# Moving normalization statistics, one normalization chain and two groups of loads in a fused deformable-convolution and mixture-of-experts kernel

## The chip, the cores and the metric

The kernel runs on one core of one Trainium2 chip. Time is the device time of one execution in microseconds (us); each version is run several times and the median is compared. The core has five engines that run side by side and wait for each other through semaphores: PE (TensorE, matmuls), DVE (VectorE), ACT (ScalarE), POOL (GpSimd) and SP (SyncE, which here only issues DMA transfers). ACT and POOL issue DMA transfers too.

## The reference, cut to what matters

Two layers on eight images of 128 channels and 64 x 64 pixels, float32. Before each layer the image is group-normalized (32 groups of 4 channels, no learned scale), and each layer's result is added to its input.

```python
# layer 0: deformable 3x3 convolution, then batch norm and relu
om = conv(_gn(x), off_w)                 # 27 maps: 9 y offsets, 9 x offsets, 9 masks
py, px = grid + offsets                  # per tap, pixel: where to sample
val = bilinear(_gn(x), py, px) * sigmoid(mask)
y = einsum('bckhw,ock->bohw', val, w) + b
x = x + relu(batch_norm(y) * gamma + beta)     # mean, var over all images
# layer 1: 4 experts, 2 chosen per image, plus a shared expert, each a 3x3 convolution
x = x + sum_e w_dense[b, e] * conv(_gn(x), expert_w[e]) + conv(_gn(x), shared_w)
```

The change touches layer 0 alone, which takes about the first 1060 us.

## The kernel before, in words

**Bands.** Each image is cut into 8 bands of 8 rows, 64 bands in all, counted by `g` through all images (`b, j = bands[g]`). The bilinear sampling is done with matrices: for each band two tables of weights, one by y offset and one by x offset, are multiplied (`weights`, L865, on DVE) to a matrix `s`; PE multiplies the transposed pixels with it (`sample`, L881, five groups per band, 12 matmuls each, so 60 in a timeline row are a whole band and 36 the three groups that PE can run ahead); ACT copies the sampled values out of PSUM (L891). PE can be three groups ahead of ACT's copies, since three PSUM buffers hold them; five `s` buffers let DVE be a band ahead of PE. Iteration `g` of the main loop first does the sampling of band `g` and then the 3x3 convolution of band `g - 1`, nine taps (L931), and between two taps it issues small pieces of everything else. A "tap" or `part` below is such a place, 0 to 8.

**Tables.** The weights come from the image's offsets. `tables(b)` is a generator that produces them for image `b`, one small step per `tick()`: four ticks per tap in the first eight iterations, three afterwards. It has two halves. The first is the normalization chain: `mv` (mean and variance per channel, made by `statistics`) goes through a matmul `pm` over the groups (L318), then on DVE `d`, `e` (L323) and `gm`, a second matmul `pv` (L328), `ve` on DVE (L333), the power −0.5 on POOL (`scale`, L336), `shift` on DVE (L339), and then the image is normalized in place in eight chunks (`pad`, L343 on ACT, L347 on DVE). The second half computes the offset convolution, writes its result to DRAM, loads it back turned by rows and by columns (ten row loads, L568; column loads, L554), nudges it (L611), forms distances (L615 for y, L626 for x), makes weights out of them with ACT (L636, L640) and a mask multiply on DVE (L673), and stores the x table (`store_x`, L591, six transfers) and the y table (`store_y`, L663) in DRAM. From there every band fetches its own part with broadcasting loads: `load_x(g)` is two transfers of 576 KB (L754), `load_y(g)` eight transfers of 36 to 144 KB (L735). These loads are issued by POOL, in the order of the program, except in the head. `spread` (L773 on ACT, L779 on DVE) turns the loaded x distances into weights. Three buffers rotate for each of the two tables.

**Statistics.** `statistics(b)` is a second generator: eight `bn_stats` (L303), one per chunk of 8 rows, and after the last one `bn_aggr` (L306), which gives `mv`. In iteration `8b + 4` it is started for image `b + 2`, whose rows are loaded by quarters (`load_quarter`) in iterations `8b + 1` to `8b + 4`. In iteration `8b + 5` what is left of the tables of image `b + 1` is run through (`for _ in made: pass`), and the chain for image `b + 2` begins.

**The head.** Up to about 95 us the tables of image 0 and the first bands are made, outside the main loop. There the loads are spread over SP, ACT and POOL. `load_y(0)` goes on SP (k = 3, 5), ACT (k = 4, 6) and POOL (the others); the y table is stored in two pieces, rows for the first band (`soon`) ahead of the loads and the rest behind them; so is the x table. `y_wts` are three y-weight buffers that must be zeroed once; the first two memsets stand earlier, the third at L990 behind `load_y(1)`.

**Order.** Each engine runs its instructions in program order. Waits are inserted by the framework from the buffers that are read and written; each DMA transfer also waits for the one before it on its lane, of which there are eight for SP and ACT together and eight for POOL.

Of the kernel before, what the change touches and what calls it, by code (L numbers as in the profile page):

```python
# [46 lines left out]
NB = NROW // 2  # L47
# [18 lines left out]
def deform_moe_conv(  # L66
# [18 lines left out]
    nc = tc.nc  # L85
    B = x.shape[0]
# [9 lines left out]
        out=gsel, in_=gsel, compare_op=ALU.is_ge, fill=0.0, base=0,  # L96
# [3 lines left out]
        out=gsel, in_=gsel, compare_op=ALU.is_ge, fill=0.0, base=3,  # L100
# [79 lines left out]
    def dense():  # L180

        with ExitStack() as st:
# [12 lines left out]
            for t in pads:  # L195
# [16 lines left out]
                out=ident, in_=ident, compare_op=ALU.is_equal, fill=0.0, base=0,  # L212
# [6 lines left out]
            for i, at in ((0, 0), (1, H - 1)):  # L219
                for half in (slice(0, W), slice(W, P)):  # L220
                    nc.gpsimd.affine_select(
                        out=nudge[half, i : i + 1], in_=nudge[half, i : i + 1],
# [16 lines left out]
            for base, sign, fill in ((-W - REACH, 1, -REACH), (P - 1 - REACH, -1, T + REACH)):  # L239
                nc.gpsimd.affine_select(  # L240
                    out=beside, in_=beside, compare_op=ALU.is_ge, fill=float(fill), base=base,
# [9 lines left out]
            raw_off = combos[1].rearrange("p h w -> p (h w)")[:, OFF_AT : OFF_AT + 18 * W].rearrange(  # L251
                "p (v t n) -> p v t n", v=3, t=2
            )
# [6 lines left out]
            y_wts = [a1.tile([P, T, 3, W, 3], F32, name=f"ywts{i}") for i in range(3)]  # L260
# [11 lines left out]
            def pause(n):  # L272
                for _ in range(n):
                    yield
# [34 lines left out]
            def tables(b):  # L309
# [4 lines left out]
                part = chunks(b)  # L314
# [42 lines left out]
                even, odd = two[:, :, 0], two[:, :, 1]  # L357
# [167 lines left out]
                for j in range(4):  # L525
                    (nc.sync if b or j % 2 == 0 else nc.scalar).dma_start(
                        out=rowwise[b][:, H // 4 * j : H // 4 * (j + 1)].rearrange(
                            "s h w -> s (h w)"
                        ),
                        in_=omr[32 * j : 32 * j + 27],  # L530
                    )
                for j in range(4):
                    (nc.sync if b or j % 2 else nc.gpsimd).dma_start(
                        out=colwise[b][:, :, j].rearrange("k u w h -> u k (w h)"),
                        in_=om[32 * j + 9 : 32 * j + 18, 1],
# [9 lines left out]
                by_row = rowwise[b].rearrange("(t k u) h w -> k h t u w", t=3, k=3)  # L545
# [3 lines left out]
                by_column = []  # L549
# [9 lines left out]
                for k in range(3):  # L559
                    lo, hi = max(0, k - 1), min(H, H + k - 1)  # L560
                    places = [(slice(lo, hi), slice(lo + 1 - k, hi + 1 - k), k)]
                    if k == 2:
                        places.append((slice(0, 1), slice(0, 1), 0))
                    if k == 0:
                        places.append((slice(H - 1, H), slice(H - 1, H), 2))
                    for outs, parts, v in places:
                        for t in range(2):
                            (nc.sync if b or t == 0 else nc.scalar).dma_start(  # L568
                                out=raw_off[parts, v, t].rearrange("p (u w) -> p u w", u=3),
                                in_=by_row[k][outs, 2 * t],  # L570
                            )
                        by_column.append((k, outs, parts, v))
                if b:
                    yield from pause(27)
                for k, *where in by_column:
# [127 lines left out]
                for k, halves in ((3, 2), (4, 2), (5, 2), (6, 2), (1, 2), (2, 2), (0, 1), (7, 1)):  # L703
                    engine = {3: nc.sync, 5: nc.sync, 4: nc.scalar, 6: nc.scalar}.get(k, nc.gpsimd)
                    for h in range(halves):
                        load_y(0, k, engine, (h,) if halves == 2 else (0, 1))
                load_x(1, nc.gpsimd)
                store_y(0, NR, slice(4 * T, H))
                store_x(4, NROW, nc.sync)
                pick(1)  # L710
# [37 lines left out]
            def load_x(g, engine):  # L748

                if g >= len(bands):  # L750
                    return
                b, j = bands[g]
                for h in range(2):
                    engine.dma_start(  # L754
                        out=x_wts[g % 3][HALF * h : HALF * h + HALF],
                        in_=bass.AP(
                            tensor=x_table[b].tensor,
                            offset=x_table[b].offset + (2 * j + h) * XROW,
                            ap=[[0, HALF], [1, XROW]],
                        ),  # L760
                    )
# [225 lines left out]
            HALVES = (0, EVEN), (EVEN, NCOL + 1)  # L987
            for k in range(2 * T):
                load_y(1, k, nc.gpsimd)
            nc.gpsimd.memset(y_wts[2], 0.0)  # L990
            load_x(2, nc.gpsimd)
            made, means_of = later, iter(())
            asked = False
# [27 lines left out]
            for g in range(len(bands) + 1):  # L1021
                b, j = bands[g] if g < len(bands) else (B, 0)
                if j == NB - 4:
                    means_of = statistics(b + 2)
                turned = pixels(g + 2)
                if j == NB - 2:
                    tick()
                for q in range(NGR):
                    if g < len(bands):
                        sample(g * NGR + q)  # L1030
                        if g:
                            weights(g * NGR + q + AHEAD)
                        if g == 0 and q == 2:
                            for k in range(Q):
                                load_y(2, k, nc.gpsimd)
                    if g == 0 and q == 1:
                        for _ in range(4):
                            next(later)
                    if q == 1:
                        put_off()  # L1040
                taps = conv(g - 1) if g else iter(())
                twice = 2 if g and bands[g - 1][1] == NB - 1 else 1
                for done, _ in enumerate(taps):
                    part, odd = divmod(done, twice)
                    if odd == 0 and part in PIXELS:
                        next(turned, None)
                    if odd == 0 and part == 2:
                        load_x(g + 3, nc.gpsimd)
                        if g < len(bands):
                            edges(g)  # L1050
                    if odd == 0 and part > 6:
                        for k in range(T * (part - 7), T * (part - 6)):
                            load_y(g + 3, k, nc.gpsimd)
                    if odd == 0 and part in SPREAD:
                        step, half = divmod(SPREAD.index(part), 2)
                        if step:
                            spread(g + 2, HALVES[half], ())
                        else:
                            spread(g + 2, sides_=(half,), clip=False)
                    if odd == 0 and part in SHARE:  # L1060
                        piece = SHARE.index(part)
                        share(g + 2, piece, MOVES[piece])
                    if odd == 0 and j == NB - 4 and part > 4:
                        next(means_of, None)
                    if odd == 0 and j == NB - 3 and part < 2:
                        for _ in range(2):
                            next(means_of, None)
                    if odd == 0 and j == NB - 3 and part == (4 if b else 7) and b + 2 < B:
                        for _ in made:
                            pass  # L1070
                        asked, made = True, tables(b + 2)
                        next(made)
                    if odd == 0 and part in BLOCKS and asked:
                        asked = False
                        tick()
                    for _ in range(3 + (g < NB) if twice == 1 else 1 + done % 2):
                        tick()
                    if odd == 0 and part == 4:
                        pick(g + 3)
                        if 2 <= j < 5:  # L1080
                            load_quarter(b + 2, j - 1)
                    if odd == 0 and part == 8 and j == 1:
                        load_quarter(b + 2, 0)
                if g == 0:
                    edges(0)
                    spread(1)
                    for n in range(AHEAD):
                        weights(NGR + n)
                for _ in turned:
                    pass  # L1090
                if g == 0:
                    for piece in range(4):
                        share(2, piece, MOVES[piece])
                    load_x(3, nc.gpsimd)
                    for k in range(Q):
                        load_y(3, k, nc.gpsimd)
                    pick(3)
                    spread(2)
                if g == 3:
                    quad_weights()  # L1100
                if j < NB - 1 and g < len(bands):
                    late.append((hand_on, g))
                xts.pop(g - 1, None)
                if j == 1 and b:
                    nc.vector.bn_aggr(ymvs[:, b - 1], ystats[:, b - 1])
                if (b, j) == (B - 1, 1):
                    reach()
# [596 lines left out]
```

## Time and profile before

| | us |
|---|---|
| median of 3 runs | 1431.47 |
| the runs | 1428.11, 1431.47, 1432.19 |
| profiled execution | 1432.73 |
| its span on the core | 1431.0 |
| PE busy / DVE busy / ACT busy / POOL busy in it | 1291.0 / 1063.3 / 835.0 / 471.6 |

The mean TensorE clock that was granted is 0.966 of full speed in the profiled execution. Times in the text are microseconds from the start of the span. In a timeline a row is a run of equal instructions on one engine: start, duration of the run, engine, line, operation, output and inputs, count, and in brackets how long the engine was idle before it and what ended that wait. The bracket is the place where lost time becomes visible; it costs something only on the engine that others wait for.

### The profile page before, as it was taken

The numbers are of one execution on the slowest core, as the hardware profiler recorded it, in microseconds if no ns is written. First come the engines' busy times: TensorE is split into PE (matmuls) and PEld (weight loads), VectorE is DVE, ScalarE is ACT, GpSimd is POOL, SyncE is SP. The second block draws the span as 40 slices with busy tenths as digits, with TensorE's granted clock in tenths as the row PEclk, the third lists the DMA queues.
The fourth block names the chain that finished last, engine by engine and source line by source line (L and its number), as shares of the span: only waits on it lengthen the run. The fifth ranks groups of instructions, "written<-read, shape, count | busy, mean of one in ns | idle before, by whom it ended". The sixth has DMA issues, their size and how long they took to land.

```text
span 1431.0 us, 21255 instructions
## 1 busy us (share of the span) xinstructions
PE 1291.0 (90%) x7561; PEld 731.3 (51%) x7561; DVE 1063.3 (74%) x2124; ACT 835.0 (58%) x1110; POOL 471.6 (33%) x750
## 2 busy tenths in 40 slices
PE   4169989999989999999998999999957999999998
PEld 1044556556656655665565565666533444444443
DVE  5658778679688778968877886746439887778972
ACT  2355866876787687688678668767623333322320
POOL 6354145335416424552552553255021110101000
PEclk9589999999999999999999999999988999999999
DMA  4589678968978887896898887689236644456411
GB/s 144 112 180 201 129 183 203 214 149 188 203 175 187 189 202 157 192 220 149 186 207 184 174 204 159 152 218 219 79 119 175 172 128 122 134 160 177 103 53 54
DMA packets 149429, 234.54 MB, mean 164 GB/s; under 512 B 101677, under 2 KB 104890, under 8 KB 139074
## 3 DMA queue, kind: packets, MB, share of 16 engines
q0 software_dynamic: 79408, 137.37, 44.4%
q1 hardware_dynamic: 69154, 95.15, 23.7%
q8 instruction: 61, 1.00, 0.3%
q10 hardware_dynamic: 752, 0.59, 0.2%
q14 instruction: 54, 0.44, 0.1%
HBM read 180.23 MB, written 45.35 MB: 158 GB/s over the span
## 4 chain that ended last, share of the span: by engine, by line
PE 54%; DMA 15%; DVE 10%; issue 9%; ACT 7%; SPq 3%; POOL 2%; DVEq 0%; ACTq 0%; POOLq 0%
PE py L931 20%; PE pc L1616 15%; PE pq L881 11%; PE pc L456 3%; DMA combo<-colwise 3%; DMA combo<-rowwise 3%; PE pt L822 3%; DMA xwts<-tabx 2%; DVE stats L303 2%; ACT xwts L773 2%; SPq L554 2%; DMA x<-in_x_dram 1%; DVE s L865 1%; DMA taby<-work 1%; DMA ywts<-taby 1%
## 5 line engine op out<-in xcount | busy, mean ns | idle before, releaser
L931 PE MATMUL py<-samples,dw_sb 128*128 128x512 f32 (+3 forms) x1296 | 561.1, 566 | 10.5 <-ACT y L939 10.5
L735 POOL DMA_DIRECT2D ywts<-taby x510 | 325.8, 656 | 386.8 <-DMA xwts<-tabx 172.4
L931 PEld LDWEIGHTS py<-samples,dw_sb 128*128 128x128 f32 x1296 | 229.8, 191 | 210.9 <-issue 175.8
L881 PE MATMUL pq<-s,xt 64*128 64x144 f32 (+1 forms) x3840 | 280.0, 299 | 35.6 <-ACT samples L891 26.7
L891 ACT COPY samples<-pq 128x864 f32<-128x864 f32 (+1 forms) x318 | 278.5, 973 | 31.4 <-PE pq L881 31.0
L881 PEld LDWEIGHTS pq<-s,xt 64*128 64x128 f32 x3840 | 254.2, 189 | 83.1 <-ACT samples L891 30.1
L865 DVE TENSOR_TENSOR s<-xwts,ywts 128x432 f32<-128x432 f32 (+1 forms) x448 | 198.6, 498 | 52.7 <-PE pq L881 41.6
L1616 PE MATMUL pc<-v,u 128*128 128x512 f32 x384 | 174.1, 600 | 6.4 <-DVE v L1523 6.3
L1616 PE MATMUL pc<-v,wmix 128*128 128x512 f32 x384 | 173.2, 596 | 0.0
L773 ACT ACTIVATE xwts<-xwts,place 128x1152 f32<-128x1152 f32 (+3 forms) x132 | 153.1, 1163 | 10.4 <-DMA xwts<-tabx 8.5
L779 DVE TENSOR_SCALAR xwts<-xwts 128x1152 f32<-128x1152 f32 (+2 forms) x128 | 96.0, 751 | 82.9 <-ACT xwts L773 82.8
L1594 ACT ACTIVATE t<-pc,bmix 128x512 f32<-128x512 f32 x32 | 22.0, 687 | 187.5 <-PE pc L1616 98.9
L754 POOL DMA_DIRECT2D xwts<-tabx x128 | 77.3, 620 | 157.1 <-DMA tabx<-combo 48.8
L939 ACT ACTIVATE y<-py,db_sb 128x512 f32<-128x512 f32 (+3 forms) x72 | 45.8, 636 | 130.0 <-PE py L931 122.9
L1616 PEld LDWEIGHTS pc<-v,u 128*128 128x128 f32 x384 | 71.8, 191 | 93.1 <-issue 83.1
L1616 PEld LDWEIGHTS pc<-v,wmix 128*128 128x128 f32 x384 | 71.9, 189 | 90.7 <-issue 89.0
L825 ACT COPY xt<-pt 128x512 f32<-128x512 f32 x126 | 74.0, 587 | 61.3 <-PE pt L822 51.3
L822 PEld LDWEIGHTS pt<-ident,picked 128*128 128x128 f32 x504 | 58.6, 141 | 91.5 <-ACT xt L825 40.3
L822 PE MATMUL pt<-ident,picked 128*128 128x128 f32 x504 | 77.8, 277 | 23.4 <-DVE picked L788 18.4
L788 DVE COPY picked<-pad 128x512 f32<-128x512 f32 x128 | 71.8, 603 | 31.2 <-PE pt L822 31.1
L838 DVE COPY xt<-xt 32x896 f32<-32x896 f32 x126 | 77.5, 615 | 2.8 <-ACT xt L825 1.2
L1012 DVE BATCH_NORM_STATS2 ystats<-y 128x6 f32<-128x512 f32 (+3 forms) x72 | 44.2, 622 | 23.7 <-ACT y L939 23.7
(209 smaller groups left out, 1168.0 us busy)
## 6 DMA issues: line engine op xcount, KB each, us to landing
xwts<-tabx POOLq DMA_DIRECT2D x128, 576.0 KB, 8.0
pad<-in_x_dram SPq DMA_DIRECT2D x36, 512.0 KB
ywts<-taby POOLq DMA_DIRECT2D x126, 144.0 KB, 9.5
out_dram<-yo SPq DMA_DIRECT2D x32, 512.0 KB
ywts<-taby POOLq DMA_DIRECT2D x126, 108.0 KB, 9.1
yd<-y SPq DMA_DIRECT2D x48, 256.0 KB
ywts<-taby POOLq DMA_DIRECT2D x126, 72.0 KB, 8.4
pad<-yd SPq DMA_DIRECT2D x16, 512.0 KB
```

What stands on the lines that cost most here:

```text
L735: engine.dma_start(out=y_wts[g % 3][HALF * h + k : HALF * (h + n) : Q, first : last + 1].rearrange("p r a b c -> p (r a b c)"), in_=bass.A ...
L754: engine.dma_start(out=x_wts[g % 3][HALF * h : HALF * h + HALF], in_=bass.AP(tensor=x_table[b].tensor, offset=x_table[b].offset + (2 * j + ...
L773: nc.scalar.activation(some, some, AF.Abs, bias=columns[side])
L779: nc.vector.tensor_scalar(some, some, -1.0, 0.0, ALU.add, ALU.min)
L822: nc.tensor.transpose(pt[:, c - c0], one.rearrange("p h x y -> p (h x y)"), ident)
L825: (nc.vector.tensor_copy if turn_odd else nc.scalar.copy)(xts[g][:, c0 : c0 + n], pt[:, 0:n])
L838: move(out=xts[g][rows, EVEN:].rearrange("p c n -> p (c n)"), in_=xts[g][rows, 1 - side : EVEN - side].rearrange("p c n -> p (c n)"),)
L865: nc.vector.tensor_tensor(s[:, :, 3 * at : 3 * (at + k)].rearrange("p m (c x) -> p m c x", x=3), by_x[:, :, c : c + k], by_y[:, :, w : w + ...
L881: nc.tensor.matmul(by_m[:, h, :, at : at + k], lhsT=xts[g][rows, c // 2 + EVEN * (c % 2)], rhs=s[rows, :, at : at + k], start=True, stop=True,
L891: (nc.scalar.copy if g or q < 3 else nc.vector.tensor_copy)(bass.AP(tensor=one.tensor, offset=one.offset + first, ap=[list(one.ap[0]), [M ...
L931: nc.tensor.matmul(py, lhsT=dw_sb[:, 3 * (2 - yy) + 2 - xx], rhs=samples[g % 2][:, m : m + 3 * n - 2 : 3, xx, 1 : W + 1], start=(i == 0), ...
L1616: nc.tensor.matmul(pc, lhsT=us[j][:, kx], rhs=vs[g][:, rows, kx : kx + W], start=(kx == 0), stop=(kx == 2),)
```

## The change

Three edits. In the row loads (L568) the list of places is made first; then the loads are issued with all the `t = 0` halves ahead of all the `t = 1` halves, and in the head they alternate between SP and ACT by place. Before, each place's two halves were issued together, `t = 0` on SP and `t = 1` on ACT; for later images all ten are on SP in both versions. In the head, `load_x(1)` moves from POOL to SP, where it follows SP's loads of y and precedes the remaining stores, and the memset of the third y-weight buffer moves from behind `load_y(1)` to the place that `load_x(1)` had. In the main loop, six of the eight statistics are issued in iteration `8b + 4` (taps 1 to 6) and two in iteration `8b + 5` (tap 0), where it was four (taps 5 to 8) and four (taps 0 and 1); and the chain of image 2 (`b` = 0) begins at tap 4, as those of the other images already did, and not at tap 7.

```diff
                     for outs, parts, v in places:
-                        for t in range(2):
-                            (nc.sync if b or t == 0 else nc.scalar).dma_start(
-                                out=raw_off[parts, v, t].rearrange("p (u w) -> p u w", u=3),
-                                in_=by_row[k][outs, 2 * t],
-                            )
                         by_column.append((k, outs, parts, v))
+                queues = (nc.sync, nc.sync if b else nc.scalar)
+                for n, t in ((n, t) for t in range(2) for n in range(len(by_column))):
+                    k, outs, parts, v = by_column[n]
+                    queues[n % 2].dma_start(
+                        out=raw_off[parts, v, t].rearrange("p (u w) -> p u w", u=3),
+                        in_=by_row[k][outs, 2 * t],
+                    )
...
-                load_x(1, nc.gpsimd)
+                nc.gpsimd.memset(y_wts[2], 0.0)
+                load_x(1, nc.sync)
                 store_y(0, NR, slice(4 * T, H))
                 store_x(4, NROW, nc.sync)
...
             for k in range(2 * T):
                 load_y(1, k, nc.gpsimd)
-            nc.gpsimd.memset(y_wts[2], 0.0)
             load_x(2, nc.gpsimd)
...
-                    if odd == 0 and j == NB - 4 and part > 4:
+                    if odd == 0 and j == NB - 4 and 0 < part < 7:
                         next(means_of, None)
-                    if odd == 0 and j == NB - 3 and part < 2:
+                    if odd == 0 and j == NB - 3 and part == 0:
                         for _ in range(2):
                             next(means_of, None)
-                    if odd == 0 and j == NB - 3 and part == (4 if b else 7) and b + 2 < B:
+                    if odd == 0 and j == NB - 3 and part == 4 and b + 2 < B:
                         for _ in made:
                             pass
                         asked, made = True, tables(b + 2)
```

## The prediction

> **What bounds the kernel now.** I read the page first (busy shares, then the chain that ended last), then the list of waits, then the timelines of the three stretches that the change touches. TensorE sets the time:
>
> ```profile
> PE 1291.0 (90%) x7561; PEld 731.3 (51%) x7561; DVE 1063.3 (74%) x2124; ACT 835.0 (58%) x1110; POOL 471.6 (33%) x750
> PE 54%; DMA 15%; DVE 10%; issue 9%; ACT 7%; SPq 3%; POOL 2%; DVEq 0%; ACTq 0%; POOLq 0%
> ```
>
> First line: busy us and share by engine. Second: the chain by engine. PE is idle for about 140 us, so a change that touches no matmul can only shorten such idle stretches. The list of waits (us in total, times, longest) names the two that matter:
>
> ```profile
> PE pq L881 <- ACT samples L891: 26.7, 16, 8.5
> PE pm L318 <- DVE mv L306: 22.6, 6, 11.5
> DVE shift L339 <- POOL scale L336: 9.2, 4, 7.9
> ```
>
> The 11.5 of mv lies in the head; the other five are 2.23 us each, one per image, at 302.73, 424.60, 544.80, 666.66 and 786.85. The timeline of PE (start, us, idle before in brackets):
>
> ```profile
> 94.92 3.49 PE L881 MATMUL pq<-s,xt 64*128 64x144 f32 x24 [8.46 <-ACT samples L891]
> 176.95 0.35 PE L318 MATMUL pm<-mv,gsel 128*128 128x1 f32 x2 [1.64 <-ACT work L636]
> 199.93 3.49 PE L881 MATMUL pq<-s,xt 64*128 64x144 f32 x24 [5.72 <-ACT samples L891]
> 424.60 0.35 PE L318 MATMUL pm<-mv,gsel 128*128 128x1 f32 x2 [2.23 <-DVE mv L306]
> ```
>
> The first row ends the head, the second and third are image 0's chain of the third image's normalization, the fourth is what images 1 to 5 pay for theirs. Their releasers, in the timelines of DVE and POOL:
>
> ```profile
> 195.26 0.16 DVE L339 SCALAR_TENSOR_TENSOR shift<-gm,scale 128x1 f32<-128x1 f32 x1 [7.89 <-POOL scale L336]
> 409.61 0.75 DVE L673 TENSOR_TENSOR work<-work,combo 64x576 f32<-64x576 f32 x1 [1.92 <-ACT work L640]
> 420.92 1.28 DVE L303 BATCH_NORM_STATS2 stats<-pad 128x6 f32<-128x512 f32 x2
> 422.77 1.27 DVE L303 BATCH_NORM_STATS2 stats<-pad 128x6 f32<-128x512 f32 x2
> 189.12 4.46 POOL L735 DMA_DIRECT2D ywts<-taby  x8 [9.04 <-DMA taby<-work]
> 194.55 0.68 POOL L336 TENSOR_TENSOR scale<-ve,nhalf 128x1 f32<-128x1 f32 x1
> ```
>
> **What the skill says.** The Trainium skill, "DMA: Bandwidth & Descriptors", section "Issuing engines are not separate DMA queues": SP, ACT and POOL transfers share 16 DMA engines, and another issuing engine saves only issue time. The trace agrees: from 60 to 80 us the DMA share is 0.99 with all three issuing, so a load moved there swaps places and shortens nothing. "TensorE: Matmul & The Clock Gate", section "Architectural detail": ACT and DVE are strictly in order, GpSimd likewise per core. Agreed: ve was ready at 187.37, but the pow (194.55) sat behind ten DMA issues on POOL. Same page, "What's actually happening": an idle window of about 3.4 us throttles PE's clock. Agreed: the 24 matmuls after the 5.72 idle took 3.49 us, 24 at 278.44 took 1.94; so joining two short waits into a long one has a price.
>
> **Part A, head row loads.** Ten SP/ACT loads are the same ten; six now go on SP and four on ACT, t=0 first. In both versions the first distance copy and the mask's sigmoid wait for all ten. Before, the last SP load issued at 41.10 and landed near 44.33; the two nudges (44.36 to 44.90) followed, the copy at 44.94. After, the nudges wait only for t=0 and are over when the last load lands, about 44.6, since it too waits for a lane freed near 41.2. Gain 0.3 us, bounds −0.3 to +0.9. In later images all ten stay on SP; the nudges again leave the end of the wait, 0.57 us of DVE.
>
> **Part B, second band's x load.** Its two DMAs (576 KB each) leave POOL, where they stood behind POOL's y loads, and go on SP behind SP's y loads; behind them on SP now stand the rest of the y table's store and three x-table stores. The 2.04 us memset (79.16) moves ahead, into POOL's waits (0.7 to 3.1 us each between 65 and 79). What bounds here is the chain: y weights 57.01 to 67.47, x-table store 67.76 to 81.43, load_x(2) issued 82.00, data until 91.28, ACT spread 91.37, PE 94.92. The engines are saturated until 80, and the same bytes must pass before the stores land. I take 0. If the x load's wait for lanes (landings near 65) delays the stores that SP issued at 65.2 to 68.4, up to +3; if y loads come earlier and the copies stop contending, −2. The memset costs nothing where POOL waits for lanes; uncovered it is 2.04.
>
> **Part C, images 1 to 5.** Eight statistics of 0.67 us: four in band 4 and four in band 5 become six and two. Between 402 and 424 the first four move up: one into a wait for ACT of 1.39 us (before the mask at 404.99), one ahead of the nudges (0.67 uncovered), two into the wait of 1.92 at 409.61, so 3 × 0.67 − 1.92 = 0.1 remains. After that two fewer (1.3 us) stand before the band's last weights, the two at 422.77 (1.27) leave, and the mask (0.66) now follows mv. mv, which ended at 424.45, ends near 424.45 + 0.1 − 1.3 − 1.27 − 0.66 = 421.3; PE reaches pm at 424.60 − 2.23 = 422.4. The wait goes: 5 × 2.23 = 11.1. What is late next: e is wanted by pv about 3 us later and follows pm at once; the pow stays behind its eight y loads, and DVE's wait for it (0.31 at 434.36) may grow by the microsecond that the rest came earlier. Nobody then feeds PE late if ACT's samples keep their lead; I keep 7.5 to 11.1.
>
> **Part C, image 0.** Here the chain also starts at the fifth tap of conv(4) instead of the eighth. First, its leftover table steps are forced out there: two masks and the y-table store come earlier, and `picked` and a clip of x weights stand before d and e. So the 1.64 wait at pm goes (mv near 172.4), but e comes only near 179.9 and PE waits about 4.3 for pv at the ninth tap: conv(4) ends near 181.1 instead of 178.22. Second, the pow now stands behind four of load_y(8)'s issues, not eight plus load_x(9)'s two, yet those four still wait for the y table's store. That landed at 188.58; its issue moves up by some 2 us but its packets run behind load_x(8)'s (180 to 185.5), so I take 187.6. Then 0.54 to the issue, four issues 2.23, pow 0.68, shift 0.2, one ACT pad 0.8, samples 1.03: PE resumes near 193. It resumes in the fourth group of band 6, though, because the pads now stand before that band's copies on ACT; before, it resumed at 199.93 in the fourth group of band 7. One band takes 191.61 − 178.22 = 13.4. So 193 + 13.4 = 206.4, a lag of 6.5; if the y store interleaves with load_x(8) and lands at 185.5, 4.4. I take +6, bounds +3 to +9. Both restarts are slow, which cancels.
>
> **Sum.** −0.3 + 0 − 11.1 + 6 = −5.4 on the profiled execution's 1432.73 (span 1431.0 and 1.7 around it), so 1427.3; it stands 1.26 above the median of the runs, from which the same sum gives 1426.1. I say 1426. A measurement can tell about 0.3%, 4.3 us: 1427.2 to 1435.8 is no change.
>
> **Rivals.**
> Image 0's stall is short (faster by more): pow is freed early because the y table lands at 184 or the copies keep PE fed; lag 0 to 2, total −9 to −11, 1421. For it: POOL is idle from 180.09 to 189.12 for that landing alone. Against: load_x(8) saturates the engines ahead of it.
> The gain is eaten (about the same): in images 1 to 5 ACT's copies or the pow become the next wait and only 6 to 8 of 11.1 stay; with +6 the total is −2 to 0, 1430. For it: POOL waits 16.4 for the y table there too. Against: shift waited only 0.31.
> Slower, one mechanism: the y table of images 1 to 5 comes late. The first four statistics now stand before the mask at 409.61 on DVE, 2.7 us of work; if nothing covers them and the masks slide by that, the y-table store (issued 422.87, landing about 428.6, after 16.36 of waiting on POOL) pushes the eight y loads, the pow behind them (433.53), shift and pads by 2.7, and ACT's copies behind the pads hold PE for it: 5 × 2.7 = 13.5, total +8.1, 1439. It decides from (5.4 + 4.3) / 5 = 1.9 us per image on. For it: shift has 0.31 of slack at most. Against: the 3.3 us of waits there, and that the last mask (422.11) loses two statistics ahead of it (1.3) for mv (0.37).
> The change doesn't do what it says: mv still comes after PE because DVE, busy 19.8 of 20 us in such stretches, slides; then each image keeps 0.5 to 1 and the whole is −1, inside "about the same".
>
> **How the numbers follow.** Sum as worked out 0.36 (two thirds of it under 1427.2), short stall 0.27, eaten or still waiting 0.17 (mostly the same), late y table, or a late head on top of the image-0 bound, 0.20. Faster 0.24 + 0.27 + 0.03 = 0.54; slower 0.20 + 0.03 = 0.23; same 0.23. The range runs from 1419 (short stall and the head's −2) to 1437 (most of the way to the late y table); the likeliest case's own is 1422 to 1430.
>
> **What would show it.** At about 300, 420, 540, 660 and 780 the pm row without its bracket (right), or with more than 1 us (wrong). Near 180 a new wait of pv for e of about 4 us; PE's long stall at about 184 to 193 with 36 matmuls of pq before it, and the scale row near 190. In the head, PE's restart at 94.92 within 2 us, the nudges ending before the row loads do. A restart after 100, or an image-0 lag at the fourth group of band 7 outside 203 to 209, makes the forecast wrong.

## The result and the profile after

The changed kernel takes 1421.91 us (median of 6 runs, 1418.81 to 1426.6), the kernel before 1431.17 (6 runs, 1428.11 to 1432.19). The ratio is 0.9938, 95% interval 0.9918 to 0.9959, so 9.3 us less. The profiled execution took 1419.31, span 1417.3, that of before 1432.73, span 1431.0; the spans of the two traces lie 13.7 us apart where the medians lie 9.3 apart. Differences between the traces are read below by place, and sizes are taken from the repeated runs.

The page of the changed kernel, busy time by engine and the chain that ended last by engine:

```profile
PE 1290.2 (91%) x7561; PEld 731.6 (52%) x7561; DVE 1063.5 (75%) x2124; ACT 834.3 (59%) x1110; POOL 477.6 (34%) x748
PE 57%; DMA 12%; ACT 12%; issue 8%; DVE 6%; POOL 3%; SPq 2%; DVEq 0%; ACTq 0%; POOLq 0%
```

PE's matmuls are the same 7561, and it is busy for 1290.2 us as before (1291.0). The two sums hide differences by place: between the starts of bands 13 and 48 (289.29 to 821.75 before, 294.04 to 811.78 after) PE is busy for 4.1 us less (509.5 and 505.3), in image 0 and the head for more. Most of what went is waiting. The list of waits (us in total, times, longest):

```profile
PE pq L884 <- ACT samples L894: 22.5, 17, 5.5
PE pm L318 <- POOL offu_sb L974: 11.5, 1, 11.5
PE pv L328 <- DVE e L323: 7.5, 3, 4.8
PE pm L318 <- DVE mv L306: 0.8, 1, 0.8
DVE shift L339 <- POOL scale L336: 14.6, 6, 6.2
```

The five waits of 2.23 us for `mv` have become one of 0.8 (the 11.5 of the head is still there, put down to another releaser). A new one of 4.8 stands at `pv`, in image 0, and DVE waits 14.6 us for the power where it waited 9.2. In images 1 to 5 little of that reaches PE: its only new waits behind it are 0.62 (at 679.49) and 0.16 (at 797.87). The timeline of PE, rows that answer to those of before:

```profile
92.18 3.49 PE L884 MATMUL pq<-s,xt 64*128 64x144 f32 x24 [5.54 <-ACT samples L894]
169.97 0.28 PE L318 MATMUL pm<-mv,gsel 128*128 128x1 f32 x2
177.81 0.59 PE L328 MATMUL pv<-e,gsel 128*128 128x1 f32 x2 [4.83 <-DVE e L323]
187.92 3.49 PE L884 MATMUL pq<-s,xt 64*128 64x144 f32 x24 [3.73 <-ACT samples L894]
422.45 0.28 PE L318 MATMUL pm<-mv,gsel 128*128 128x1 f32 x2
```

The head ends at 92.18 instead of 94.92. In image 0 `pm` no longer waits, but `pv` does, and the long stall has moved from the fourth group of band 7 (199.93) to that of band 6 (187.92). In image 2's turn (422.45) `pm` has no bracket. DVE and POOL around these places:

```profile
185.93 0.16 DVE L339 SCALAR_TENSOR_TENSOR shift<-gm,scale 128x1 f32<-128x1 f32 x1 [6.20 <-POOL scale L336]
403.74 0.70 DVE L303 BATCH_NORM_STATS2 stats<-pad 128x6 f32<-128x512 f32 x1
421.28 0.37 DVE L306 BATCH_NORM_AGGREGATE mv<-stats 128x2 f32<-128x48 f32 x1
...
183.08 2.24 POOL L738 DMA_DIRECT2D ywts<-taby  x4 [8.95 <-DMA taby<-work]
185.30 0.60 POOL L336 TENSOR_TENSOR scale<-ve,nhalf 128x1 f32<-128x1 f32 x1
```

`mv` starts at 421.28, 1.2 us before PE asks for it. The power (185.30) stands behind four loads that waited 8.95 us for the y table.

### The profile page after: what moved, and what is told of

It is laid out like the page before. It is cut to its first block, busy times and chain, and to the rows that moved or that the text cites. A ratio compares the mean times of both kernels' runs of the same rounds, so it can differ in the third digit from the quotient of the medians.

```text
span 1417.3 us, 21259 instructions
## 1 busy us (share of the span) xinstructions
PE 1290.2 (91%) x7561; PEld 731.6 (52%) x7561; DVE 1063.5 (75%) x2124; ACT 834.3 (59%) x1110; POOL 477.6 (34%) x748
## 4 chain that ended last, share of the span: by engine, by line
PE 57%; DMA 12%; ACT 12%; issue 8%; DVE 6%; POOL 3%; SPq 2%; DVEq 0%; ACTq 0%; POOLq 0%
PE py L934 21%; PE pc L1618 17%; PE pq L884 11%; DMA ywts<-taby 3%; PE pc L456 3%; PE pt L825 3%; ACT xwts L776 2%; DMA combo<-colwise 2%; ACT work L638 2%; DMA pad<-in_x_dram 1%; ACT samples L894 1%; DMA x<-in_x_dram 1%; DVE s L868 1%; POOL ywts L738 1%; ACT xt L841 1%
## 5 line engine op out<-in xcount | busy, mean ns | idle before, releaser
L934 PE MATMUL py<-samples,dw_sb 128*128 128x512 f32 (+3 forms) x1296 | 555.1, 561 | 9.7 <-ACT y L942 9.7
L738 POOL DMA_DIRECT2D ywts<-taby x510 | 335.0, 671 | 368.0 <-DMA xwts<-tabx 151.8
L934 PEld LDWEIGHTS py<-samples,dw_sb 128*128 128x128 f32 x1296 | 226.8, 189 | 206.8 <-issue 174.2
L884 PE MATMUL pq<-s,xt 64*128 64x144 f32 (+1 forms) x3840 | 284.4, 302 | 29.8 <-ACT samples L894 22.5
L884 PEld LDWEIGHTS pq<-s,xt 64*128 64x128 f32 x3840 | 257.6, 191 | 78.6 <-ACT samples L894 26.9
L757 POOL DMA_DIRECT2D xwts<-tabx x126 | 73.5, 590 | 164.3 <-DVE samples L911 34.9
```

Source lines behind the costliest of these rows:

```text
L738: engine.dma_start(out=y_wts[g % 3][HALF * h + k : HALF * (h + n) : Q, first : last + 1].rearrange("p r a b c -> p (r a b c)"), in_=bass.A ...
L757: engine.dma_start(out=x_wts[g % 3][HALF * h : HALF * h + HALF], in_=bass.AP(tensor=x_table[b].tensor, offset=x_table[b].offset + (2 * j + ...
L884: nc.tensor.matmul(by_m[:, h, :, at : at + k], lhsT=xts[g][rows, c // 2 + EVEN * (c % 2)], rhs=s[rows, :, at : at + k], start=True, stop=True,
L934: nc.tensor.matmul(py, lhsT=dw_sb[:, 3 * (2 - yy) + 2 - xx], rhs=samples[g % 2][:, m : m + 3 * n - 2 : 3, xx, 1 : W + 1], start=(i == 0), ...
```

## Where the time came from

The starts of PE's sampling matmuls, which are the same 3840 in every version, set the traces side by side (us from the start of the span; "band 7, fourth group" is the place where the prediction measured image 0's lag; images and bands are counted from 0):

| start of | before | after | difference |
|---|---|---|---|
| band 0 | 72.99 | 69.84 | -3.2 |
| band 5, fourth group | 165.29 | 162.73 | -2.6 |
| band 7, fourth group | 199.93 | 203.68 | +3.8 |
| band 13, fourth group | 293.10 | 296.47 | +3.4 |
| band 48 | 821.75 | 811.78 | -10.0 |
| band 63, fourth group | 1037.14 | 1022.41 | -14.7 |

Head -2.6; image 0 +5.9 (from -2.6 to +3.4); images 1 to 5 -13.3 (to -10.0). The last step, -4.8, lies far from every edit: it falls between the starts of bands 56 and 57, where PE finishes image 6's convolution. Its last 18 matmuls, before, after, and in the trace of the x load alone (an experiment below):

```profile
949.77 6.94 PE L931 MATMUL py<-samples,dw_sb 128*128 128x256 f32 x18 [3.44 <-ACT y L939]
```

```profile
937.77 4.22 PE L934 MATMUL py<-samples,dw_sb 128*128 128x256 f32 x18 [1.39 <-ACT y L942]
```

```profile
944.80 4.22 PE L931 MATMUL py<-samples,dw_sb 128*128 128x256 f32 x18 [1.38 <-ACT y L939]
```

This step goes with the place of the second band's x load in the head. In the eight traces with that load on SP (the changed kernel and seven experiments) bands 56 and 57 start 15.74 or 15.75 us apart, with a wait of 1.38 or 1.39 here. In the six with it on POOL (the kernel before and five experiments) the distance is 15.75 in one and 16.57 to 20.75 in the others, 18.96 in the mean, with waits of 1.39 to 4.42. So it is, on average, worth 3.2 us. How a load in the head reaches as far as this is not shown, and there is one trace of each kernel. The trace of before, with 20.51 here and a late head (see the row loads below), lies above its kind at both places, which is part of why two single traces differ by more than the medians.

More than 11.1 came out of images 1 to 5. The trace of before shows why. PE's rows after two of the five waits:

```profile
302.73 0.35 PE L318 MATMUL pm<-mv,gsel 128*128 128x1 f32 x2 [2.23 <-DVE mv L306]
302.94 4.54 PE L931 MATMUL py<-samples,dw_sb 128*128 128x512 f32 x6
...
424.81 2.88 PE L931 MATMUL py<-samples,dw_sb 128*128 128x512 f32 x6
```

The same six matmuls (three taps, two each) took 4.54 us after the wait at 302.73 and 2.88 after the wait of the same length at 424.60. The granted clock was 0.61 of full speed in the first stretch (302.9 to 307.3) and 1.00 in the second (424.8 to 427.6). In three of the five images (4.54, 4.53, 4.43) the wait was followed by slow matmuls, in two (2.88, 2.88) it wasn't. So the bracket was not the whole price: 1.55 to 1.66 us more in three images, 4.9 together. In the trace of after all five take 2.87 or 2.88. The bands that follow these places start 3.1 (image 1, which keeps 0.8), 2.5, 4.1, 2.5 and 4.1 us earlier, 16.3 in all; 0.6 to 1.1 us is lost again later in each of images 2 to 5, and 13.3 remains.

The other traces agree. From band 13's fourth group to band 48 the six kernels with the statistics of before take 527.0 to 528.9 us, the eight with the new ones 514.4 to 515.3, whatever else they have. Of the 30 places with the old statistics 17 show the slow matmuls (4.12 to 4.54), two or three in each trace and not always in the same images; of the 40 with the new ones none does.

## The experiments

Each was made from the kernel before or from the changed one, and compared with the kernel before on the same chip; its median in the three groups of runs was 1429.89, 1427.93 and 1429.72. The question was whether the parts add, and what each is worth alone.

**Row loads alone.** The whole first hunk of the diff, of which the core is:

```diff
-                            (nc.sync if b or t == 0 else nc.scalar).dma_start(
+                queues = (nc.sync, nc.sync if b else nc.scalar)
+                for n, t in ((n, t) for t in range(2) for n in range(len(by_column))):
+                    queues[n % 2].dma_start(
```

> Part A alone: the row loads in the new order and on the new queues, everything else as before. Theory (the parts add): the first distance copy, which was at 44.94 us, comes 1.1 us earlier, as it did with the whole change (43.80), and PE's restart at 94.92 by as much; the whole time is 1.1 us lower (0.9992 of before). Rival (part A needs part B): the x-table store stays bound by the saturated transfers between 60 and 80 us, the restart stays within 0.4 us of 94.92 and the time is the same.

Measured 1428.71 (13 runs), ratio 1.0003 (0.999 to 1.0016): no change. In its trace the copy came at 43.16 us and the restart at 93.11. The nudges do leave the end of the wait:

```profile
40.77 0.54 DVE L613 TENSOR_SCALAR combo<-combo,nudge 64x192 f32<-64x192 f32 x2 [1.49 <-DMA combo<-rowwise]
43.16 0.81 DVE L617 COPY combo<-combo 64x576 f32<-64x576 f32 x1 [1.85 <-DMA combo<-rowwise]
```

But heads with no edit at all (in the traces of the statistics, of the chain, and of both) restarted at 93.39 to 93.53, too: the 94.92 of the one trace of before is late for its own kernel, and neither the theory's nor the rival's place of the restart means much against it. Over all traces the copy comes at 43.1 to 44.7 in the seven with the new row loads, 43.7 in the mean, and at 43.2 to 44.9 in the seven without, 44.0 in the mean. The time doesn't show a gain; its interval leaves from 1.4 us less to 2.3 more, so neither the theory's 1.1 nor the 0.3 of the prediction is ruled out.

**The x load and the memset, together and apart.** The first line is the memset's edit (it goes from behind the y loads of band 1), the others are the x load's:

```diff
+                nc.gpsimd.memset(y_wts[2], 0.0)
-                load_x(1, nc.gpsimd)
+                load_x(1, nc.sync)
```

> Part B alone: the second band's x load on SP behind SP's y loads, the memset of the third y-weight buffer ahead of POOL's loads for band 1. Theory (the parts add): PE's first samples come about 2 us earlier than 72.99, since band 0's y loads no longer share the engines with that x load, and the restart at 94.92 comes 1.6 us earlier; time 1.6 us lower. Rival: the head's gain is all part A's, the restart stays within 0.4 us of 94.92.

Measured 1426.49 (6 runs), 0.9974 (0.9961 to 0.9988): 3.7 us, more than the 1.6 that was expected.

> The kernel before, with the second band's x load on SP and the memset left where it was. Theory (the x load's place makes part B's gain, since band 0's y loads stop sharing the engines with it): 3 us of part B's 3.7 remain, 0.998. Rival (the memset of 2.04 us at 79.16, just ahead of band 2's x load, was not hidden): the time is the same as before, 0.9995 to 1.001.

Measured 1425.52 (22 runs), 0.9974 (0.9961 to 0.9986).

> The kernel before, with the memset moved ahead of POOL's loads and the x load left on POOL. Theory (the memset lay in the shadow of the x-table store, whose landing at 81.43 released the next load at 82.00): same, 0.9995 to 1.001. Rival: 2 us, 0.9986.

Measured 1430.34 (14 runs), 1.0007 (0.9995 to 1.0019).

The x load's place makes the whole of part B, 3.7 us, and the memset was hidden. A part of it is seen in the head. The first samples of band 0 come earlier. PE in the trace of the x load alone:

```profile
69.97 6.66 PE L881 MATMUL pq<-s,xt 64*128 64x216 f32 x60 [5.35 <-DVE s L865]
```

It was 72.99 with a wait of 7.61 before. In the six traces with the x load on POOL the first samples started between 71.16 and 72.99, in the eight with it on SP between 69.23 and 70.84; there is no overlap. The same bytes pass in another order, and band 0's y weights come out ahead: from the issue of band 0's x loads to the landing of the last of its y loads on POOL it took 16.2 us in the trace of before, and 14.0 with the x load alone on SP. At PE's restart (91.14 to 94.12 with, 92.34 to 94.92 without, means 92.6 and 93.5) only about 0.9 us of that remains. The other place where the traces differ by this load is the end of image 6's convolution shown above, 3.2 us in the mean. The two together are about as large as the 3.7, but only the first has a mechanism that is seen.

**Statistics and chain together, without the head's edits.**

```diff
-                    if odd == 0 and j == NB - 4 and part > 4:
+                    if odd == 0 and j == NB - 4 and 0 < part < 7:
-                    if odd == 0 and j == NB - 3 and part < 2:
+                    if odd == 0 and j == NB - 3 and part == 0:
-                    if odd == 0 and j == NB - 3 and part == (4 if b else 7) and b + 2 < B:
+                    if odd == 0 and j == NB - 3 and part == 4 and b + 2 < B:
```

> Part C alone: statistics six and two, image 2's chain at the fifth tap. Theory: images 1 to 5 lose the wait of PE for mv (2.23 us each, 11.1) and, where the clock had been throttled after it (4.53 instead of 2.88 us for the next six taps, in three of the five), another 1.65 each, 5 in all; image 0 gives back about 6 by the fourth group of band 7, of which some is regained: total -7 to -10 us, 0.993 to 0.995 of before. Rival: image 0's loss stays in full and the throttled clock returns elsewhere, -5 us (0.9965).

Measured 1424.0 (6 runs), 0.9962 (0.995 to 0.9974), -5.4 us: the rival's -5. What I had expected to be regained of image 0's loss was not, in the measure of the repeated runs. The next runs take the two edits apart.

**The chain of image 2 back at tap 7.** The changed kernel with one line undone:

```diff
-                    if odd == 0 and j == NB - 3 and part == 4 and b + 2 < B:
+                    if odd == 0 and j == NB - 3 and part == (4 if b else 7) and b + 2 < B:
```

> The whole change, except that image 2's chain begins at tap 7 again, as before. Theory (the earlier chain costs image 0 about 6 us): PE's wait for pv near 178 us (4.83) is gone, the fourth group of band 7 comes 3 to 6 us earlier than the 203.59 of the whole change, and the time is 4 to 6 us under the whole change's 1421.9: 1416 to 1418, ratio to before about 0.990. Rival (what the earlier chain loses around 180 us comes back at the end of image 0, since the tables of image 2 are earlier): band 9 starts where it did and the time is within 2 us of the whole change.

Measured 1411.07 (4 runs, 1410.58 to 1412.68), 0.987 (0.9855 to 0.9885). Repeated with a later group of runs:

> The whole change with image 2's chain at tap 7 once more, beside the version before on the same chip, so that the two can be compared. Every theory: 0.987 of before, as measured.

Measured 1411.91 (6 runs), 0.9873 (0.9854 to 0.9893). So the earlier chain costs the changed kernel 0.0065 to 0.0068 of 1430, 9.3 to 9.7 us, and the version without it is the best one measured, 18 us under the kernel before. That is more than the 4 to 6 us that were expected of this line. PE in image 0 of the first of the two:

```profile
172.27 0.28 PE L318 MATMUL pm<-mv,gsel 128*128 128x1 f32 x2
...
181.69 0.34 PE L328 MATMUL pv<-e,gsel 128*128 128x1 f32 x2
...
194.36 2.83 PE L884 MATMUL pq<-s,xt 64*128 64x144 f32 x24 [4.43 <-ACT samples L894]
```

No wait at `pm`, none at `pv`, and the stall is back in band 7, with 4.43 us where the kernel before had 5.72. Against this trace the changed kernel is 0.7 us ahead at band 1's fourth group, 9.3 behind at band 7's (3 to 6 were expected), 13.5 at band 8, 9.0 at band 9, and 9.9 behind at band 16, from where on the two run side by side.

**Statistics alone, and the chain alone, in the kernel before.** The first two pairs of lines of the diff above for statistics and chain together, and its third pair.

> Statistics six and two alone; image 2's chain at tap 7 and the head's loads as before. Theory (the parts add; the earlier chain costs 10.8 us, as the runs with and without it showed): -5.4 - 10.8 = -16 us, 0.989 of before. Rival (the gain needs the head's loads in their new place): less than -12 us.

Measured 1414.59 (5 runs), 0.9894 (0.987 to 0.9919), 15 us: the theory's.

> The kernel before with one edit, image 2's chain at tap 4; statistics four and four. Theory (the loss of image 0 is the earlier chain's own): PE waits for mv near 171 to 176 us for about 5 us, then for pv, then behind the power; +10 to +13 us, 1.008 of before. Rival (the early chain loses only together with the early statistics): within 3 us of before.

Measured 1439.02 (6 runs), 1.0076 (1.005 to 1.0103), 10.9 us more: the theory's, though the wait for `mv` was 3.68 and not 5:

```profile
175.19 0.55 PE L318 MATMUL pm<-mv,gsel 128*128 128x1 f32 x2 [3.68 <-DVE mv L306]
175.61 5.47 PE L931 MATMUL py<-samples,dw_sb 128*128 128x512 f32 x6
...
188.23 3.34 PE L881 MATMUL pq<-s,xt 64*128 64x144 f32 x24 [3.48 <-ACT samples L891]
```

Thus the parts add within their intervals: statistics -15, chain +10.9 make -4, measured -5.4; with the head's -3.7 it is about -8 to -9, measured -9.3 (0.9938 of 1430 is -8.9).

**The power ahead of the y loads, chain at tap 4.** The changed kernel, all eight loads of band 8 at tap 8 of iteration 5:

```diff
-                    if odd == 0 and part > 6:
-                        for k in range(T * (part - 7), T * (part - 6)):
+                    if odd == 0 and part > (6, 7)[g == NB - 3]:
+                        for k in range(0 if g == NB - 3 else T * (part - 7), T * (part - 6)):
                             load_y(g + 3, k, nc.gpsimd)
```

> The whole change, and in iteration 5 all eight loads of band 8's y weights are issued at tap 8 and none at tap 7, so that image 2's power stands ahead of them on POOL and waits for no y table. Theory (of the 10.8 us that the earlier chain costs, the stall behind the power is 3.73 us of waiting and 1.55 us of throttled matmuls): the power comes near 180 instead of 185.30, PE's long wait of band 6 goes, the wait for pv (4.83) stays; -5 us against the whole change, near 1417. Rival (the y loads and not the power set that restart): no change, 1422, with a wait of the same length for another releaser.

Measured 1412.81 (5 runs), 0.9894 (0.9867 to 0.992), about 6 us better than the whole change. POOL and PE in its trace:

```profile
179.89 0.98 POOL L336 TENSOR_TENSOR scale<-ve,nhalf 128x1 f32<-128x1 f32 x1 [5.08 <-DVE ve L333]
184.07 4.57 POOL L738 DMA_DIRECT2D ywts<-taby  x8 [3.20 <-DMA taby<-work]
```

```profile
178.52 0.59 PE L328 MATMUL pv<-e,gsel 128*128 128x1 f32 x2 [4.83 <-DVE e L323]
180.96 5.44 PE L884 MATMUL pq<-s,xt 64*128 64x216 f32 x60
```

The power waits for `ve` instead of for a transfer, band 6 runs through without a stall, and the wait of 4.83 for `pv` stays. That splits the loss: some 6 us is the power's place on POOL; 3 to 4 remain, and the wait for `pv`, with the slow matmuls behind it (5.44 us for a band's samples that take 4.20 elsewhere), is what remains in the trace. That this wait makes those 3 to 4 was not tried by itself.

**The same for the chain at tap 7.** Two tries to improve the best version. In the first, the eight loads go from taps 7 and 8 of iteration 5 to tap 4 of iteration 6 (all lines but the last); in the second, band 9's x load goes from tap 2 of iteration 6 to behind them as well (the last line). The lines that take the loads out of their old places are left out here:

```diff
                     for _ in range(3 + (g < NB) if twice == 1 else 1 + done % 2):
                         tick()
+                    if g == NB - 2 and part == 4:
+                        for k in range(2 * T):
+                            load_y(g + 2, k, nc.gpsimd)
+                        load_x(g + 3, nc.gpsimd)
```

> The whole change with image 2's chain at tap 7, and band 8's y loads moved from taps 7 and 8 of iteration 5 to tap 4 of iteration 6, behind the power. Theory: the power comes near 182.6 instead of 188.98, shift and the four pads on ACT are over near 188, and the wait of 4.43 us in the fourth group of band 7 and most of the throttled matmuls behind it (2.83 and 1.85 instead of 1.94 and 1.04) go: -5 to -6 us against the 1411.1 of the version with the late y loads not moved, 1405 to 1406. Rival: the y weights of band 8 now come too late and PE waits as long one band later; 1410 or more.

Measured 1412.43 (5 runs), 0.9887 (0.9862 to 0.9913): the rival. The stall of band 7 went, and another came:

```profile
206.23 5.30 PE L456 MATMUL pc<-combo,offu_sb 128*32 128x256 f32 x48 [7.34 <-DVE combo L421]
```

```profile
198.52 1.27 DVE L868 TENSOR_TENSOR s<-xwts,ywts 128x432 f32<-128x432 f32 x3 [10.80 <-DMA ywts<-taby]
```

DVE stood 10.80 us at band 8's weights, whose y loads were issued at 187.49, and behind them in its queue were the combinations that PE needed for the offset convolution.

> As the version with the chain at tap 7 and the y loads of band 8 behind the power, but band 9's x load is also moved, from tap 2 of iteration 6 to behind those y loads, so that the y table's store isn't held up by two x loads. Theory (in that version the store landed near 187 instead of 183 because two x loads of 1.18 MB ran ahead of it, and the first weights of band 8 then waited 10.80 us for y loads): the y loads are issued near 183.5 again, the power stays near 182, the weights of band 8 come near 194 and PE waits 1 to 3 us instead of 7.34 for the combination matmuls near 200; 2 to 4 us under the version with the chain at tap 7 alone. Rival (the y loads' own time sets the weights of band 8, whatever stands before them): no better than that version.

Measured 1414.65 (6 runs), 0.9896 (0.9872 to 0.992): the rival again. The y loads were issued from 184.30 on, but DVE still waited 11.78 us at band 8's weights, put down to an x transfer, and PE 8.45 at the same matmuls:

```profile
209.16 4.75 PE L456 MATMUL pc<-combo,offu_sb 128*32 128x256 f32 x48 [8.45 <-DVE combo L421]
```

In both, the power is out of PE's way, and the table loads of band 8 then come last. Whether these or the x load beside them set that wait was not taken further apart.

## Why the prediction was right

The time (1421.9) lies in the range (1419 to 1437) and the direction is the one that was forecast; the point, 1426, was 4 us too high. By the steps of its sum:

- **Part C, images 1 to 5** (-11.1): right in mechanism and in the place of each instruction. `mv` was to end near 421.3 and ended at 421.65; `pm` runs without a wait in four of the five. The size was off: 13.3 in the trace. The missed term is the throttled clock after three of the five waits, 4.9 us. The prediction saw this clock in 3.49 against 1.94 us, yet counted only brackets here. It had named the Trainium skill for it, "TensorE: Matmul & The Clock Gate", section "What's actually happening", which has the clock fall after an idle window of about 3.4 us. This case's traces differ: waits of 2.23 us, shorter than that, were followed by the lower clock in more than half of the places, and the measurement decides.
- **Part C, image 0** (+6): right in place, mechanism and sum, and the sum by two errors that cancel. The lag at the fourth group of band 7, the head's -2.6 taken off, is 6.3. `pv` waited 4.83 where 4.3 was said. The step that put the power behind four loads that wait for the y table is shown by the run that took them from ahead of it. But the restart was worked out as 193 and came at 187.92, 190.5 with the head's 2.6 added: the table landed 2.5 us earlier than was taken (near the 185.5 of the prediction's own lower case). And the band behind it, taken as 13.4, took 15.8 (187.92 to 203.68), since its first matmuls are throttled (3.49 us, granted clock 0.50) and the restart of before, which comes later, doesn't cancel that at the place compared. Seen from the other side the price is larger than 6: with the chain left at tap 7 the other edits would have gained 9.3 to 9.7 us more, since image 0 gains by the early statistics too (3.1 us in the trace of the statistics alone, from band 5's fourth group to band 13).
- **Part B** (0, bounds -2 to +3): wrong in size. The step "the same bytes must pass before the stores land" may hold for the engines, but first samples depend on which bytes pass first. A load moved to another issuing engine "swaps places and shortens nothing", the prediction concluded; the swap itself was worth 3.7 us (2.0 to 5.6), more than the -2 that it allowed for y loads that come earlier. Only 0.9 of it is seen at the end of the head, which is where the prediction looked. That the memset costs nothing was right (1.0007).
- **Part A** (-0.3, bounds -0.3 to +0.9 of gain): the mechanism is as said, since the nudges come ahead of the copy's wait, and the copy is 0.3 us earlier in the mean of the traces, though the two sets overlap. In the time it can't be told from nothing.
- **The sum**: by the repeated runs part C as a whole measured -5.4 (-3.7 to -7.2), where the sum has -11.1 + 6 = -5.1, and part B -3.7, where it has 0. So the 4 us by which the point was off are the size of part B's. That part C came so near is in part luck: image 0's two errors cancel, and in the traces of before and after it makes more (13.3 - 5.9 = 7.4, just beyond the interval).
- The rivals: the short stall was not what happened, nor was PE held by a late y table. (In image 2's turn POOL's y loads were issued at 428.35, 429.12 before; DVE's wait for the power grew from 0.31 to 1.77, about the microsecond that the prediction allowed, and PE didn't wait for it.) The changed time is near that of the short stall for another reason, the x load.
- **Its signs**: the `pm` rows without brackets (in four images of five), the wait of `pv` and the lag at band 7's fourth group (203.68) came as said. The restart in the head came 2.7 us earlier and not within 2, and the stall of image 0 ended at 187.92 and not at 193, with `scale` at 185.30 and not near 190.

## What to carry to other kernels

An instruction of 0.6 us on an in-order queue that also issues loads takes the time of whatever those loads wait for: look at what stands ahead of it before moving its chain. Price a wait of PE as the bracket and the matmuls behind it, by comparing the duration of equal rows. And when a change has three parts, run each alone: here one of them took away half of what the others brought.

## What the runs showed that was not expected

Equal waits of 2.23 us were followed by slow matmuls in three images and not in two, in one execution: the six matmuls took 4.43 to 4.54 us or 2.88. The moment of the first samples in the head varies by 1.8 us (71.16 to 72.99) between kernels whose x load was the same, more than part A was meant to bring. And the place of one x load in the head goes with a step of up to 5 us some 870 us later (15.75 against up to 20.75 between two band starts), for which no mechanism was found.
